# Four of 32 neighbour rows copied as columns of a turned table in SBUF, and a fifth fetched row by row by SyncE in two tiles of three

## The chip, the core and the metric

The kernel runs on one core of a Trainium2 chip. The metric is the device time of one execution in microseconds (us), of which the median over several runs is given. A core has five engines that run their own instruction queues beside each other: TensorE (PE in the profile), VectorE (DVE), ScalarE (ACT), GpSimd (POOL) and SyncE (SP). SP issues DMA transfers and computes nothing; POOL issues the indirect ones, whose source rows are named by a list of indices in SBUF.

## What is computed

The reference scores each of 16,384 users by a history of 100 items. Ahead of that, for each of 50,001 items and two tables of 32 values, it attends over the rows of the item's 32 neighbours:

```python
def _neighbor_attn(E, near_full):
    V = E[near_full]                      # [items, 32 neighbours, 32]
    scores = jnp.einsum('nd,nkd->nk', E, V) / jnp.sqrt(jnp.float32(GEO_HALF))
    w = jax.nn.softmax(scores, axis=-1)
    return jnp.einsum('nk,nkd->nd', w, V)
a_sus = _neighbor_attn(E_in, near_full)
a_inf = _neighbor_attn(E_out, near_full)
```

Then come the user scores, over rows `[E_hist, a_sus, a_inf]` of the history and `[E_tgt, a_inf, a_sus]` of the target, a hidden layer of 128 with relu, an exponential with a mask, a weighted sum over everything and a sigmoid for each user. All of it is in float32.

## The kernel before, in words

There are two stages, one after the other.

The item stage works on the rows of `egeo`, which has both tables side by side: 64 values, 256 bytes an item, `ROWS` = 50,048 items with the padding. A tile is 128 items, one in each partition; 17 tiles (`NSUB`) form an iteration, and there are 23 iterations, `NT` = 391 tiles. `load` brings an iteration's neighbour lists (`nidx`), own rows (`own`) and `ehist` rows (`row`) by SP; it is called in the middle of the iteration before. `gather(s)` issues 32 indirect transfers on POOL for tile s, one for each neighbour number k: each brings 128 rows of 64 values into `v[:, k]`. `v` has five buffers.

The arithmetic of a tile is spread over three steps of the loop over s. The loop writes out the order of the instructions on ACT, DVE and SP by hand (`manual_schedule`). In step s, DVE first does the weighted sum of tile s-2 (`weighted` twice, `attend`, `attended`), then the products and scores of tile s-1 (`products`, `scores`, `largest`). ACT copies the own rows of tile s-1 into PSUM (`even`) and takes the exponents of its scores (`exponents`). `finish(s-3)` completes a row, and at the end of an iteration writes the finished rows to two tables in DRAM (`table`, `ttab`) through ACT's queue.

The user stage follows: for each of 128 groups of 128 users and each of 100 places in the history, POOL gathers 128 rows of `table` (`h`), TensorE turns them, DVE multiplies them by the target's row, TensorE and ACT do the hidden layer and TensorE the scores. The change doesn't touch it.

In step s of the item stage the order is:

```python
gather(s)
if two:
    weighted(s - 2, 0); weighted(s - 2, 1); attend(s - 2); attended(s - 2)
if one:
    even(s - 1); products(s - 1); scores(s - 1); largest(s - 1); exponents(s - 1)
if three:
    finish(s - 3)
```

Of the kernel before, what the change touches and what calls it, by code (L numbers as in the profile page):

```python
# [22 lines left out]
DE = 64  # L23
# [8 lines left out]
NSUB = 17  # L32
NITER = -(-ITEMS // (P * NSUB))
ROWS = NITER * P * NSUB

# [17 lines left out]
def kernel(  # L53
# [13 lines left out]
    nc = tc.nc  # L67

    const = ctx.enter_context(tc.tile_pool(name="const", bufs=1))
# [31 lines left out]
    nc.scalar.dma_start(ttab[0 : ITEMS - 1, 0:DE], etgt[0 : ITEMS - 1, :])  # L104
    nc.scalar.dma_start(ttab[ITEMS - 1 : ITEMS, 0:DE], etgt[ITEMS - 1 : ITEMS, :])
    with (
        tc.manual_schedule(engines={E.Activation, E.DVE, E.SP}),
        tc.tile_pool(name="n_in", bufs=2) as n_in,
        tc.tile_pool(name="n_v", bufs=5) as n_v,
        tc.tile_pool(name="n_s", bufs=3) as n_s,  # L110
        tc.tile_pool(name="n_ps", bufs=2, space=bass.MemoryType.PSUM) as n_ps,
        tc.tile_pool(name="n_pb", bufs=1, space=bass.MemoryType.PSUM) as n_pb,
    ):
        its = {}
        subs = {}

        def load(it):
            nidx = n_in.tile([P, NSUB, K], I32, name="nidx")
            nc.sync.dma_start(nidx, near_v[it])
            own = n_in.tile([P, NSUB, 2 * G], F32, name="own")  # L120
            nc.sync.dma_start(own, egeo_v[it])

            row = n_in.tile([P, NSUB, W + G], F32, name="row")
            nc.sync.dma_start(row[:, :, 1 : 1 + DE], ehist_v[it])

            its[it] = (nidx, own, row)

        def gather(s):  # L130
            it, j = divmod(s, NSUB)
            nidx = its[it][0]
            v = n_v.tile([P, K, 2, G], F32, name="v")
            subs[s].update(v=v)
            for k in range(K):
                nc.gpsimd.indirect_dma_start(  # L136
                    out=v[:, k].rearrange("p t d -> p (t d)"),
                    out_offset=None,
                    in_=egeo,
                    in_offset=bass.IndirectOffsetOnAxis(ap=nidx[:, j, k : k + 1], axis=0),  # L140
                )

        def even(s):
            it, j = divmod(s, NSUB)
            own_ps = n_ps.tile([P, 1, 2 * G], F32, name="own_ps")
            nc.scalar.copy(own_ps[:, 0, :], its[it][1][:, j, :])
            subs[s]["own"] = own_ps

        def products(s):
            v = subs[s]["v"]  # L150
            prod = n_pb.tile([P, K * 2 * G], F32, name="big")
            prod = prod.rearrange("p (k t d) -> p k t d", k=K, t=2)
            nc.vector.tensor_tensor(  # L153
                prod.rearrange("p k t d -> p k (t d)"),
                v.rearrange("p k t d -> p k (t d)"),
                subs[s]["own"].to_broadcast([P, K, 2 * G]),
                ALU.mult,
            )
            subs[s]["prod"] = prod

        def scores(s):
            sc = n_s.tile([P, 2, K], F32, name="sc")
            nc.vector.tensor_reduce(  # L163
                sc.rearrange("p t k -> p k t"), subs[s]["prod"], AX.X, ALU.add
            )
            subs[s]["sc"] = sc

        def largest(s):
            sc = subs[s]["sc"]
            top = n_s.tile([P, 2], F32, name="top")  # L170
            nc.vector.tensor_reduce(top, sc, AX.X, ALU.max)
            nc.vector.tensor_scalar(top, top, -scale, None, ALU.mult)  # L172
            subs[s]["sc"] = (sc, top)

        def exponents(s):
            sc, top = subs[s]["sc"]
            ex = n_ps.tile([P, 2, K], F32, name="ex")
            tot = n_s.tile([P, 2, 1], F32, name="tot")
            for t in range(2):
                nc.scalar.activation(  # L180
                    ex[:, t, :],
                    sc[:, t, :],
                    AF.Exp,
                    bias=top[:, t : t + 1],
                    scale=scale,
                    accum_out=tot[:, t, :],
                )
# [14 lines left out]

        def attend(s):
            tot = subs[s]["ex"][1]
            nc.vector.reciprocal(tot, tot)
            att = n_s.tile([P, 2, G], F32, name="att")
            nc.vector.tensor_reduce(att, subs[s]["wv"], AX.X, ALU.add)  # L207
            subs[s]["att"] = att
# [12 lines left out]
        def finish(s):  # L221
            it, j = divmod(s, NSUB)
            row = its[it][2]
            nc.scalar.copy(row[:, j, W : W + G], row[:, j, 1 + DE : 1 + DE + G])
# [12 lines left out]

        NT = NITER * NSUB
        load(0)
        for s in range(NT + 3):  # L240
            if s < NT:
                if s % NSUB == NSUB // 2 and s // NSUB + 1 < NITER:
                    load(s // NSUB + 1)
                subs[s] = {}
                gather(s)
            one, two, three = (0 <= s - d < NT for d in (1, 2, 3))
            if two:
                weighted(s - 2, 0)
                weighted(s - 2, 1)
                attend(s - 2)  # L250
                attended(s - 2)
# [186 lines left out]
    with (  # L438
# [5 lines left out]
        part = f_s.tile([P, UC], F32, name="part")  # L444
# [6 lines left out]
        s = f_s.tile([P, 1], F32, name="s")  # L451
# [72 lines left out]
```

## Time and profile before

| what | value |
|---|---|
| median of 3 runs | 36178.12 us (36170.38 to 36182.2) |
| span of the profiled execution, first to last instruction | 31861.9 us |
| POOL busy | 24005.6 us, 25446 instructions |
| DVE busy | 6716.4 us |
| PE busy | 11868.8 us, nearly all in the user stage |
| mean granted TensorE clock | 0.905 |

The median lies 4316 us above the span of the profiled execution. The profile gives no time of that execution other than its span.

The profile is one execution as the hardware recorded it. A row of a group of instructions reads: line, engine, operation, output<-inputs, partitions x elements, count | busy us, mean ns of one | idle us of the engine just before them, and what ended most of it. A row of the timeline reads: start in us, duration in us, engine, line, operation, count [idle before it <- what ended it]. "SPq" is SP's queue of transfers. A row of waits reads: engine, tile and line <- what ended the wait: us in total, times, longest. "PEld" is TensorE's loading of weights.

### The profile page before, as it was taken

To read this page: it belongs to the slowest core of one execution; us is meant where nothing else is said; L and a number is where in the kernel's file an instruction comes from. 1 tells how busy PE (TensorE), PEld (TensorE's weight loads), DVE (VectorE), ACT (ScalarE), POOL (GpSimd) and SP (SyncE) were. 2 spreads that over 40 slices of the span, in tenths; PEclk is the share of its full clock that TensorE was granted. 3 is DMA by queue.
4 is the path that set the end of the run, shared out by engine and by line. 5 is a ranking of instruction groups with operands and counts; after the bars stand their busy time and mean duration, and the time that the engine had idled before them with its cause. 6 is when DMAs were issued, how large, how long until landed. Compare 5 with 4: busy or idle time off the path is not lost.

```text
span 31861.9 us, 106268 instructions
## 1 busy us (share of the span) xinstructions
PE 11868.8 (37%) x26243; PEld 3178.4 (10%) x26243; DVE 6716.4 (21%) x11111; ACT 2745.2 (9%) x6067; POOL 24005.6 (75%) x25446
## 2 busy tenths in 40 slices
PE   0000000000000000000277777777777777777777
PEld 0000000000000000000011111111111111111111
DVE  2222222222222222222211111111111111111111
ACT  0000000000000000000011111111111111111111
POOL 7777777777777777777777777777777777777777
PEclk9999999999999999999988888888888888888888
DMA  2111111111111111111122222222222222222222
GB/s 50 30 30 30 30 31 33 30 30 30 30 31 33 30 30 30 30 31 31 37 54 54 54 54 54 54 54 54 54 54 54 54 54 54 54 54 54 54 53 52
DMA packets 1027971, 1362.44 MB, mean 43 GB/s; under 512 B 559904, under 2 KB 614432, under 8 KB 1027360
## 3 DMA queue, kind: packets, MB, share of 16 engines
q0 software_dynamic: 814080, 1265.42, 19.7%
q10 hardware_dynamic: 151056, 51.51, 1.0%
q1 hardware_dynamic: 62224, 38.72, 0.5%
q8 instruction: 217, 3.56, 0.0%
q14 instruction: 394, 3.23, 0.0%
HBM read 1315.31 MB, written 51.50 MB: 43 GB/s over the span
## 4 chain that ended last, share of the span: by engine, by line
POOL 56%; issue 27%; DMA 9%; PE 7%; DVE 1%; POOLq 0%; ACT 0%; ACTq 0%; SPq 0%; DVEq 0%
POOL v L136 35%; POOL h L332 21%; DMA h<-table,hidx 6%; PE turned L372 3%; DMA v<-in_egeo_dram,nidx 3%; PE z_ps L363 3%; PE hT_ps L346 1%; POOL t L296 0%; DVE xT L351 0%; DVE ea L404 0%; DVE den L403 0%; DVE num L405 0%; DVE ea L402 0%; DVE hsum L354 0%; DMA table<-row 0%
## 5 line engine op out<-in xcount | busy, mean ns | idle before, releaser
L332 POOL DMA_INDIRECT h<-table,hidx x12800 | 12080.4, 944 | 3901.8 <-issue 3587.3
L136 POOL DMA_INDIRECT v<-in_egeo_dram,nidx x12512 | 11803.8, 943 | 3860.2 <-issue 3723.3
L308 PE MATMUL hT_ps<-ident,t 128*128 128x128 f32 x128 | 46.7, 365 | 15689.8 <-DMA hidx<-in_history_dram 15689.8
L346 PE MATMUL hT_ps<-ident,h 128*128 128x128 f32 x12800 | 3926.4, 350 | 4284.2 <-DMA h<-table,hidx 4186.4
L351 DVE TENSOR_TENSOR xT<-hT_ps,tT 128x512 f32<-128x512 f32 x3200 | 2213.9, 692 | 13113.0 <-PE hT_ps L346 13109.7
L372 PE MATMUL turned<-z,w_row 128*25 128x512 f32 x6400 | 4560.1, 805 | 0.0
L363 PE MATMUL z_ps<-xT,w1T 128*128 128x512 f32 x6400 | 4300.2, 761 | 0.0
L365 ACT ACTIVATE z<-z_ps,b_sb 128x512 f32<-128x512 f32 x3200 | 2199.7, 687 | 13823.9 <-PE z_ps L363 13823.9
L153 DVE TENSOR_TENSOR big<-v,own_ps 128x2048 f32<-128x2048 f32 x391 | 897.9, 2296 | 11251.8 <-DMA v<-in_egeo_dram,nidx 11251.5
L346 PEld LDWEIGHTS hT_ps<-ident,h 128*128 128x128 f32 x12800 | 1779.4, 154 | 9334.4 <-DMA h<-table,hidx 5701.4
L308 PEld LDWEIGHTS hT_ps<-ident,t 128*128 128x128 f32 x128 | 19.2, 150 | 15842.7 <-issue 15841.9
L180 ACT ACTIVATE ex<-sc,top 128x32 f32<-128x32 f32 x782 | 227.7, 291 | 15155.2 <-DVE top L172 15142.5
L363 PEld LDWEIGHTS z_ps<-xT,w1T 128*128 128x128 f32 x6400 | 1343.1, 255 | 3.1 <-ACT z L365 3.1
L194 DVE TENSOR_TENSOR big<-v,ex 128x1024 f32<-128x1024 f32 x782 | 960.6, 1228 | 355.5 <-ACT ex L180 342.0
L163 DVE TENSOR_REDUCE sc<-big 128x64 f32<-128x2048 f32 x391 | 896.4, 2293 | 13.4
L207 DVE TENSOR_REDUCE att<-big 128x64 f32<-128x2048 f32 x391 | 895.8, 2291 | 0.0
L372 PEld LDWEIGHTS turned<-z,w_row 128*25 128x25 f32 x6400 | 458.8, 115 | 3323.6 <-issue 3323.6
L354 DVE COPY hsum<-h 128x4 f32<-128x4 f32 x3200 | 528.5, 165 | 0.0
L296 POOL DMA_INDIRECT t<-ttab,tidx x128 | 120.8, 943 | 66.0 <-issue 37.8
L180 ACT ACTIVATION_READ_ACCUMULATOR ex<-sc,top 128x1 f32 x782 | 145.8, 186 | 0.0
L310 DVE COPY tT<-hT_ps 128x128 f32<-128x128 f32 x128 | 37.4, 292 | 262.4 <-PE hT_ps L308 262.4
L214 DVE TENSOR_TENSOR row<-att,tot 128x64 f32<-128x64 f32 x391 | 88.2, 226 | 13.3
(55 smaller groups left out, 1008.1 us busy)
## 6 DMA issues: line engine op xcount, KB each, us to landing
h<-table,hidx POOLq DMA_INDIRECT x12800, 2.6
v<-in_egeo_dram,nidx POOLq DMA_INDIRECT x12512, 2.4
table<-row ACTq DMA_DIRECT2D x22, 1096.5 KB, 13.4
own<-in_egeo_dram SPq DMA_DIRECT2D x23, 544.0 KB, 4.0
row<-in_ehist_dram SPq DMA_DIRECT2D x23, 544.0 KB, 4.9
ttab<-in_etgt_dram ACTq DMA_DIRECT2D x1, 12500.0 KB, 54.2
ttab<-row ACTq DMA_DIRECT2D x22, 544.0 KB, 4.6
hidx<-in_history_dram SPq DMA_DIRECT2D x32, 200.0 KB, 2.5
```

The costliest lines, as they stand in the source:

```text
L136: nc.gpsimd.indirect_dma_start(out=v[:, k].rearrange("p t d -> p (t d)"), out_offset=None, in_=egeo, in_offset=bass.IndirectOffsetOnAxis(a ...
L153: nc.vector.tensor_tensor(prod.rearrange("p k t d -> p k (t d)"), v.rearrange("p k t d -> p k (t d)"), subs[s]["own"].to_broadcast([P, K, ...
L163: nc.vector.tensor_reduce(sc.rearrange("p t k -> p k t"), subs[s]["prod"], AX.X, ALU.add)
L194: nc.vector.tensor_tensor(subs[s]["wv"][:, t].rearrange("p d k -> p k d"), subs[s]["v"][:, :, t, :], subs[s]["ex"][0][:, t, :] .rearrange( ...
L207: nc.vector.tensor_reduce(att, subs[s]["wv"], AX.X, ALU.add)
L332: nc.gpsimd.indirect_dma_start(out=rows[s][:, q, :], out_offset=None, in_=table, in_offset=bass.IndirectOffsetOnAxis(ap=users[c]["hidx"][: ...
L346: nc.tensor.transpose(hT[s][:, q, :], rows[s][:, q, 1:W], ident)
L351: nc.vector.tensor_tensor(xT[s], hT.pop(s), users[c]["tT"].to_broadcast([D, LG, P]), ALU.mult)
L354: copy = nc.vector.tensor_copy(users[c]["hsum"][:, g * LG : (g + 1) * LG], rows.pop(s)[:, :, 0:1].rearrange("p q o -> p (q o)"),)
L363: nc.tensor.matmul(z_ps, w1T, xT.pop(s), start=True, stop=True)
L365: nc.scalar.activation(z[s], z_ps, AF.Relu, bias=b1_sb)
L372: nc.tensor.matmul(users[c]["turned"], w2_row[:, NG - 1 - g : 2 * NG - 1 - g], of.rearrange("h q p -> h (q p)"), start=g == 0, stop=g == N ...
```

## The change

Tables of columns. `cols`, 128 partitions x 25,088 values (98 KB a partition), is laid out in SBUF. In partitions 0 to 63 its column i holds the 64 values of item i, in partitions 64 to 127 those of item i + 25,088 (`HALF`). `table_of_columns` fills it during the first six tiles (`WARM`): SP loads blocks of 128 rows, TensorE turns them, and DVE and ACT by turns copy 512 columns out of PSUM.

Addresses. Once in an iteration `addresses` turns the numbers of the last five neighbours (k = 27 to 31) of each item into byte addresses: a row's offset in DRAM for k = 27, a column's address in SBUF for the others, with `mark` telling the half. TensorE turns them, so that a tile's 128 addresses for one k lie in one partition, where a sequencer can load 16 of them into registers at once (`RUN`).

From tile 6 on, `gather(s)` issues 28 indirect transfers, or 27 where s is not divisible by three. The four columns k = 28 to 31 of a tile are 512 single columns of 128 values: DVE copies 256 of them (`by_dve`, k = 28 and 29), ACT 224, and TensorE the last 32 as products of the identity with one column (`by_pe`, two runs, `PEB`), which ACT then copies out of PSUM. `Columns.some` loads the registers of the next run before it issues the 16 copies of the present one. In the next step TensorE turns the 4 x 128 columns back into rows (`turned`), ACT copies the lower half's 64 values into `v` (`lower`), and DVE overwrites those of items in the upper half (`upper`, a predicated copy).

In two tiles of three SP fetches the rows of k = 27 one by one (`single_rows`): 128 transfers of 256 bytes, the source address in a register.

The work is interleaved by hand: `products`, `scores` and `attend` are cut into two parts each, and a run of 16 copies of DVE stands behind each of the eight large operations; the other eight runs follow at the end of the step. ACT does two runs, `lower` and `even`, eight runs, `exponents`, and the last four runs. `own` and `ex` share one PSUM tile, since the new tiles `vt` and `pc` take PSUM banks.

Built, the program has 1,796 indirect transfers fewer on POOL (10,716 in the item stage), 98,560 copies of one column more on DVE, 86,240 on ACT, 12,320 products of one column on TensorE, 14,368 loads of 16 registers, and 32,768 transfers of one row on SP. The transfers of SP use eight semaphores in turn: each waits until the one eight places before it has landed.

```diff
+HALF = -(-ROWS // (2 * P)) * P
+KC = 4
+KS = K - KC - 1
+KA = KC + 1
+RUN = 16
+WARM = 6
+PEB = 2
...
+        def columns_at(eng, s, q):
+            it, j = divmod(s, NSUB)
+            k, i = divmod(q * RUN, P)
+            r = j * KA + 1 + k
+            _, vals = nc.values_load_multi_w_load_instructions(
+                marks[it][1][r : r + 1, i : i + RUN],
+                engines=[eng],
...
+        def single_rows(s):
...
+            for i in range(0, P, RUN):
+                _, vals = nc.values_load_multi_w_load_instructions(
+                    marks[it][1][r : r + 1, i : i + RUN],
+                    engines=[E.SP],
...
+                for q, a in enumerate(vals):
...
+                    nc.sync.dma_start(
+                        v[i + q : i + q + 1, KS].rearrange("p t d -> p (t d)"),
+                        flat[:, ds(a // 4, DE)],
+                    )
+
+        class Columns:
...
+            def some(self, n=1):
+                for _ in range(n):
+                    if self.ready is None:
+                        if not self.runs:
+                            return
+                        self.ready = (self.runs[0], columns_at(self.eng, self.s, self.runs.pop(0)))
+                    q, vals = self.ready
+                    self.ready = None
+                    if self.runs:
+                        self.ready = (self.runs[0], columns_at(self.eng, self.s, self.runs.pop(0)))
+                    for i, a in enumerate(vals):
+                        self.put(q, i, a)
...
-            for k in range(K):
+            for k in range(K if s < WARM else KS if fetched(s) else KS + 1):
                 nc.gpsimd.indirect_dma_start(
...
+        def fetched(s):
+            return s >= WARM and s % 3 != 0
...
+        def turned(s):
+            vt = n_pc.tile([P, 4, P], F32, name="vt")
+            for k in range(KC):
+                nc.tensor.transpose(vt[:, k, :], subs[s]["cb"][k // 2][:, k % 2, :], ident)
+            subs[s]["vt"] = vt
+
+        def lower(s):
+            nc.scalar.copy(
+                subs[s]["v"][:, K - KC : K].rearrange("p k t d -> p k (t d)"),
+                subs[s]["vt"][:, :, 0:DE],
+            )
...
+            def by_dve(q, i, a):
+                k, o = divmod(q * RUN + i, P)
+                nc.vector.tensor_copy(cb[0][:, k, o : o + 1], cols[:, ds(a, 1)])
+
+            def by_act(q, i, a):
+                k, o = divmod(q * RUN + i - 2 * P, P)
+                nc.scalar.copy(cb[1][:, k, o : o + 1], cols[:, ds(a, 1)])
+
+            def by_pe(q, i, a):
+                o = (q - (2 * half - PEB)) * RUN + i
+                nc.tensor.matmul(
+                    pc[:, 0, o : o + 1], ident, cols[:, ds(a, 1)], start=True, stop=True
+                )
...
+            late = one and s - 1 >= WARM
+            if late:
+                turned(s - 1)
+            if WARM <= s < NT:
+                dve, act, pe = columns(s)
+            pe.some(PEB)
+            act.some(2)
+            if late:
+                lower(s - 1)
             if one:
                 even(s - 1)
-                products(s - 1)
-                scores(s - 1)
+            act.some(8)
+            if two:
+                for t in range(2):
+                    weighted(s - 2, t)
+                    dve.some()
+                for t in range(2):
+                    attend(s - 2, t)
+                    dve.some()
+                attended(s - 2)
+            if late:
+                upper(s - 1)
+            if one:
+                for part in range(2):
+                    products(s - 1, part)
+                    dve.some()
+                for part in range(2):
+                    scores(s - 1, part)
+                    dve.some()
                 largest(s - 1)
                 exponents(s - 1)
+            act.some(99)
+            dve.some(99)
+            if WARM <= s < NT and PEB:
+                n = PEB * RUN
+                nc.scalar.copy(subs[s]["cb"][1][:, 1, P - n : P], subs[s]["pc"][:, 0, 0:n])
```

More of the change, by code (lines that the diff above doesn't have):

```diff
@@ L106 @@
     with (
-        tc.manual_schedule(engines={E.Activation, E.DVE, E.SP}),
+        tc.manual_schedule(engines={E.Activation, E.DVE, E.SP, E.PE}),
+        tc.tile_pool(name="n_e", bufs=6) as n_e,
+        tc.tile_pool(name="n_c", bufs=2) as n_c,
         tc.tile_pool(name="n_in", bufs=2) as n_in,
@@ new lines, in columns_at @@
+        def columns_at(eng, s, q):
[5 more added lines that the diff above has]
+                engines=[eng],
+                min_val=base,
+                max_val=base + 4 * (HALF - 1),
+                skip_runtime_bounds_check_because="an item's number within its half, times 4",
+            )
+            return [
+                (
+                    v.with_bounds(
+                        min_val=base,
+                        max_val=base + 4 * (HALF - 1),
+                        guaranteed_mod_val=0,
+                        out_of_modulus=4,
+                    )
+                    - base
+                )
+                // 4
+                for v in vals
+            ]
@@ L141, in gather @@
                 )
+        def fetched(s):
+            return s >= WARM and s % 3 != 0
         def even(s):
             it, j = divmod(s, NSUB)
[L145 to L149, printed above, removed]
-            v = subs[s]["v"]
-            prod = n_pb.tile([P, K * 2 * G], F32, name="big")
-            prod = prod.rearrange("p (k t d) -> p k t d", k=K, t=2)
+            oe = n_ps.tile([P, 2, 2 * G], F32, name="oe")
+            nc.scalar.copy(oe[:, 0, :], its[it][1][:, j, :])
+            subs[s]["own"] = oe[:, 0:1, :]
+            subs[s]["ex_ps"] = oe[:, 1, :].rearrange("p (t k) -> p t k", t=2)
@@ L153, in products @@
+        def products(s, part):
+            v = subs[s]["v"]
+            if part == 0:
+                big = n_pb.tile([P, K * 2 * G], F32, name="big")
+                subs[s]["prod"] = big.rearrange("p (k t d) -> p k t d", k=K, t=2)
+                subs[s]["sc"] = n_s.tile([P, 2, K], F32, name="sc")
+            ks = slice(part * K // 2, (part + 1) * K // 2)
             nc.vector.tensor_tensor(
-                prod.rearrange("p k t d -> p k (t d)"),
-                v.rearrange("p k t d -> p k (t d)"),
@@ L201, in weighted, with attend @@
             )
[L203 to L208, printed above, removed]
+        def attend(s, t):
+            if t == 0:
+                tot = subs[s]["ex"][1]
+                nc.vector.reciprocal(tot, tot)
+                subs[s]["att"] = n_s.tile([P, 2, G], F32, name="att")
+            nc.vector.tensor_reduce(
+                subs[s]["att"][:, t : t + 1], subs[s]["wv"][:, t : t + 1], AX.X, ALU.add
+            )
         def attended(s):
@@ L238, with columns, some @@
         NT = NITER * NSUB
+        groups = -(-blocks // 4)
         load(0)
+        def columns(s):
+            cb = [n_c.tile([P, 2, P], F32, name=n) for n in ("cd", "ca")]
+            subs[s]["cb"] = cb
+            half = 2 * P // RUN
+            pc = n_pc.tile([P, 4, P], F32, name="pc")
+            subs[s]["pc"] = pc
+            def by_dve(q, i, a):
[8 more added lines that the diff above has]
+                    pc[:, 0, o : o + 1], ident, cols[:, ds(a, 1)], start=True, stop=True
+                )
+            return (
+                Columns(E.DVE, s, range(half), by_dve),
+                Columns(E.Activation, s, range(half, 2 * half - PEB), by_act),
+                Columns(E.PE, s, range(2 * half - PEB, 2 * half), by_pe),
+            )
+        class Nothing:
+            def some(self, n=1):
+                pass
         for s in range(NT + 3):
+            dve = act = pe = Nothing()
             if s < NT:
```

106 lines of the change are left out of this document (94 added, 12 removed).

## The prediction

> **What bounds the kernel now.** I read the page first: busy shares, then the chain of waits.
>
> ```profile
> span 31861.9 us, 106268 instructions
> PE 11868.8 (37%) x26243; PEld 3178.4 (10%) x26243; DVE 6716.4 (21%) x11111; ACT 2745.2 (9%) x6067; POOL 24005.6 (75%) x25446
> POOL 56%; issue 27%; DMA 9%; PE 7%; DVE 1%; POOLq 0%; ACT 0%; ACTq 0%; SPq 0%; DVEq 0%
> L136 POOL DMA_INDIRECT v<-in_egeo_dram,nidx x12512 | 11803.8, 943 | 3860.2 <-issue 3723.3
> ```
>
> POOL is busy for 75%, and most of the rest of the chain is "issue", the gap in which POOL waits for nothing. The item stage's gathers are L136. Their timeline gives what one costs with its gap:
>
> ```profile
> 9.88 1.10 POOL L136 DMA_INDIRECT v<-in_egeo_dram,nidx  x1 [8.57 <-DMA nidx<-in_near_dram]
> ...
> 15664.44 0.94 POOL L136 DMA_INDIRECT v<-in_egeo_dram,nidx  x1 [0.30 <-issue]
> ```
>
> 12,511 steps in 15,654.56 us are 1.2513 us each; 32 make a tile of 40.04 us. The waits and the windows show that the other engines follow:
>
> ```profile
> DVE big L153 <- DMA v<-in_egeo_dram,nidx: 11251.5, 390, 30.3
> ACT ex L180 <- DVE top L172: 15142.5, 391, 39.6
> 60.00:15660.00 15600.00, 0.00 (x0) 0.00 (x0) 3947.88 (x3531) 410.16 (x2338) 11761.74 (x12468) 1.00 0.17 31
> ```
>
> The windows' columns are PE, PEld, DVE, ACT, POOL. Over 390 tiles DVE works 10.12 us and ACT 1.05 us a tile, and PE nothing. DVE waits 28.9 us a tile for gathers. This idle time is what the change spends.
>
> **What is removed.** From tile 6 on, POOL gathers 28 columns in tiles divisible by three (129 tiles) and 27 in the other 256: 10,716 gathers in place of 12,512. 1,796 x 1.2513 = 2,247 us, if POOL stays the bound. POOL's mean over the 385 tiles becomes 27.34 x 1.2513 = 34.2 us. Every other engine has to stay below 34.2 a tile for the whole gain, and below 40.04 for any.
>
> **DVE.** 256 copies of 128x1 a tile with the source column in a register, 16 loads of 16 registers, a predicated copy, and three big operations cut in two. No row has a register address. The nearest is the small copy L354:
>
> ```profile
> L354 DVE COPY hsum<-h 128x4 f32<-128x4 f32 x3200 | 528.5, 165 | 0.0
> 15889.42 0.16 DVE L354 COPY hsum<-h 128x4 f32<-128x4 f32 x1
> 15889.49 0.26 DVE L402 TENSOR_TENSOR ea<-ea,keep 128x100 f32<-128x100 f32 x1
> L310 DVE COPY tT<-hT_ps 128x128 f32<-128x128 f32 x128 | 37.4, 292 | 262.4 <-PE hT_ps L308 262.4
> ```
>
> It lasts 0.165 us, but the next operation starts 0.07 us after it: neighbours overlap. Bounds: 0.07 and 0.165. I take 0.07, since the copies depend on nothing and stand in rows of 16: 17.9 us. The fixed work becomes 10.1 + 3 x 0.07 + about 0.45 (predicated copy of 256 elements out of PSUM, by L310 and 128 elements more) + 0.3 (the address work, once in 17 tiles) = 11.1 us.
>
> **The register loads.** No row shows one. Below stands a sequencer's own instruction, above the shortest landing of a DMA:
>
> ```profile
> L292 SPq EVENT_SEMAPHORE  x148: 17/28/1356, 15667.0 to 29818.4; - x148
> L292 SPq DMA_DIRECT2D hidx<-in_history_dram x32: 327/328/617, 15692.2 to 29819.7; - x32
> out_dram<-res SPq DMA_DIRECT2D x1, 64.0 KB, 1.6
> ```
>
> So 0.03 to 1.6 us. I take 0.45, nearest to the 0.33 us in which SP's sequencer handles one transfer, plus something for the read. Each load is for the next run; on DVE eight of 16 stand behind an operation of about 1.1 us, which hides them; without that cover they cost 3.6 us more. The other eight cost 3.6. DVE: 17.9 + 11.1 + 3.6 = 32.6 us; ends 29.2 (loads nearly free) to 66 (0.165 a copy, eight loads at 1.6 us).
>
> [...]
>
> **ACT.** 224 copies, 14 loads, a copy of 256 elements out of PSUM and one of 32.
>
> ```profile
> 6025.01 0.20 ACT L224 COPY row<-row 128x32 f32<-128x32 f32 x1
> 6025.12 0.20 ACT L146 COPY own_ps<-own 128x64 f32<-128x64 f32 x1
> L382 ACT COPY by_g<-turned 25x512 f32<-25x512 f32 x128 | 71.5, 558 | 2.9 <-PE turned L372 2.9
> ```
>
> Spacing 0.11 (a 32-element copy), length 0.20: 24.6 to 45 us; I take 0.11. With 1.05 + 0.35 + 0.2 fixed and 14 x 0.45 of loads: 32.5 us. What is new behind a wait: `exponents` stands after ten runs and waits for DVE's `largest`; behind it wait four runs, the copy of PE's columns and `finish`, and for these PE's turning of the next step. DVE reaches `largest` after 8 runs (9.0) and nearly all fixed work, at about 20 us of its step; ACT's ten runs end at about 17.6 + 4.5 = 22. The wait is late for nobody.
>
> **PE.** 32 one-column products and four turnings.
>
> ```profile
> L450 PE MATMUL s_ps<-psum,ones 128*128 128x1 f32 x2 | 0.6, 346 | 6.2 <-DVE psum L448 6.2
> L450 PEld LDWEIGHTS s_ps<-psum,ones 128*128 128x128 f32 x2 | 0.5, 309 | 6.2 <-issue 6.2
> ```
>
> 36 x (0.35 + 0.31) = 24 us at most, on an engine idle here. Hidden; uncovered it would be added to ACT's 32-column copy and the turning.
>
> **SP.** In 256 tiles 128 transfers of one row, and 8 loads with nothing in front of them.
>
> ```profile
> 0.75 0.38 SPq L85 DMA_DIRECT2D b_sb<-in_b_dram  x1
> 1.19 0.42 SPq L87 DMA_DIRECT2D w_sb<-in_w_dram  x1
> 1.66 0.55 SPq L89 DMA_DIRECT2D w_sb<-in_w_dram  x1
> ```
>
> These rows start 0.44 and 0.47 us apart; L292 above takes 0.33. Those have 128 rows to describe, the new ones one, so 0.47 is the upper bound; the lower is 0.2, since in the built program each transfer waits for the one eight before it to land, and the shortest landing is 1.6 us. I take 0.37 (L292 and a gap of 0.04): 47.4 + 3.6 = 51 us, over three tiles two of these, 34.0 a tile. The ends are 17 (0.2, loads at 0.03) and 49 (0.47, loads at 1.6). Five `v` buffers let SP run ahead in the tile without rows, so that the mean over three tiles counts. SP's loads of `nidx`, `own` and `row` now queue behind the rows, but are issued nine tiles before their use, some 300 us; a late one would stop POOL and, in `addresses`, DVE.
>
> **Tables at the start.** 98 transfers, 196 transposes and 49 PSUM copies of 512 elements run beside six tiles of 40 us; by L382 25 copies are 14 us an engine. Hidden; uncovered some 30 us.
>
> **Sum.** POOL 34.2, SP 34.0, DVE 32.6, ACT 32.5: POOL still sets the pace, but by very little. The profiled span becomes 31,862 - 2,247 = 29,615, plus about 70 us for steps in which one of four nearly equal engines comes late: 29,685. The median of 36,178 stands 4,316 above the profiled span; no row shows this time, so I leave it as it is: 36,178 - 2,177 = **34,000 us**. Were it spread in proportion (36,178 / 31,862 = 1.1355), the gain would be 2,551 and the time 33,627. A measurement here can tell 0.2% (72 us) from no change.
>
> **Rivals.**
> 1. The pace passes to one of the other three, short of 40.04. At 36.5 us a tile the gain is 3.5 x 385 = 1,360: 34,820. For it: three sums within 2 us of POOL's. Against: each would have to be well above its nearest row.
> 2. Slower: DVE's register copies can't be started ahead like L354's. It decides from (40.04 - 11.1 - 3.6) / 256 = 0.099 us a copy, midway between spacing and length. At 0.115: 44.1 us, + 1,560: 37,740; at 0.165 and no overlap 56.9 us: 42,700. For it: no row shows such an instruction. ACT's own point is (40.04 - 7.9) / 224 = 0.143.
> 3. Slower by the loads: each holds its sequencer for the 1.6 us landing and nothing hides it: 16 x 1.6 + 17.9 = 43.5 us, with the big operations beside the loads: + 1,330, 37,510. [...]
> 4. No gain: SP's transfers keep the 0.44 us spacing: (56.3 + 3.6) x 2/3 = 39.9 us: 36,140.
> 5. The change doesn't do what it says: gathers get dearer beside DVE's many copies. From 1.465 us (40.04 / 27.34) nothing is left. Against: L332 runs beside L354 in the second stage at the same 0.94.
>
> ```profile
> L332 POOL DMA_INDIRECT h<-table,hidx x12800 | 12080.4, 944 | 3901.8 <-issue 3587.3 <-PE turned L372 159.1 <-PE hT_ps L346 97.8
> ```
>
> **How the numbers follow.** Forecast 0.40 (33,550 to 34,500), rival 1 0.23, rival 2 0.24, rival 3 0.07, rivals 4 and 5 0.06, of which 0.04 are no change. Faster: 0.40 + 0.23 + 0.01 = 0.64; same 0.04; slower 0.32. Below 33,550 I leave 0.02; the upper end at 37,500 takes in rivals 1, 4 and the mild half of 2 and leaves 0.17.
>
> **What will show it.** L136's successor with 10,716 gathers, still 1.25 us apart with "issue" before them, and POOL first in the chain: right. Gathers that wait for DVE or ACT to free `v`: rival 1 or 2; then the spacing of the 128x1 copies decides (0.07 or above 0.099), and any hole of over 0.5 us between runs is the load. A wait of `products` for SP's rows points to SP. The first 240 us and the second stage should look as before. Wrong altogether: gathers above 1.4 us.

## The result, and the profile after

| | runs | median us | lowest to highest |
|---|---|---|---|
| before | 4 | 36,178.12 | 36,170.38 to 36,182.2 |
| after | 4 | 44,176.83 | 44,133.84 to 44,222.77 |

The ratio is 1.2212, with a 95% interval of 1.2194 to 1.2229: the change makes the kernel 22% slower, and the predicted 34,000 us is 10,200 us off. The page of the profiled execution of the changed kernel (44,210.67 us), with busy time and mean length of one behind the bar, and idle time and what ended it last:

```profile
span 44208.5 us, 432721 instructions
PE 15785.9 (36%) x52642; PEld 8822.8 (20%) x52642; DVE 13938.0 (32%) x111416; ACT 12380.8 (28%) x93101; POOL 22308.3 (50%) x23650
L267 POOL DMA_INDIRECT v<-in_egeo_dram,nidx x10716 | 10110.0, 943 | 15299.6 <-DVE big L353 12017.1
L416 ACT COPY ca<-cols 128x1 f32 x86240 | 9483.7, 187 | 13676.4 <-issue 13595.4
L412 DVE COPY cd<-cols 128x1 f32 x98560 | 7315.0, 145 | 11213.0 <-issue 10623.1
```

POOL is down from 75% to 50%. A gather still takes 943 ns, there are 10,716 of them as planned, and yet POOL stands idle for 15,300 us before them, mostly until DVE has done its last product of an older tile and a `v` buffer is free. So DVE is late. But DVE is busy for only 32%, and what it waits for before its small copies is "issue": nothing that the profile shows. ACT has the same.

Before the two traces are compared, one number of the prediction has to be put right. The page shown there had a span of 31,862 us, the timed runs 36,178. A second execution of the unchanged kernel, profiled beside the experiments below, took 36,322 us, like the timed ones. Its page and its windows (columns PE, PEld, DVE, ACT, POOL, granted clock, DMA share, GB/s):

```profile
span 36320.2 us, 106268 instructions
L136 POOL DMA_INDIRECT v<-in_egeo_dram,nidx x12512 | 13320.4, 1065 | 4176.0 <-issue 4081.4
```

```profile
0.00:17510.00 17510.00, 0.45 (x1) 0.18 (x1) 3960.95 (x3543) 412.77 (x2346) 13321.05 (x12518) 1.00 0.16 28
17510.00:36320.00 18810.00, 10060.81 (x26242) 3152.57 (x26242) 2734.17 (x7569) 2295.83 (x3721) 12197.40 (x12928) 0.73 0.21 46
```

The 4,316 us are inside the program, in both stages, and not around it. The item stage ends at 17,500 us instead of 15,665; its gathers are 1.398 us apart in the mean, where the first page had 1.251. All that follows is compared with this execution. The same windows for the changed kernel:

```profile
0.00:25500.00 25500.00, 5783.44 (x26332) 5682.13 (x26332) 11175.40 (x103564) 10060.76 (x89173) 10110.72 (x10722) 0.50 0.10 19
25500.00:44208.00 18708.00, 10002.44 (x26310) 3140.65 (x26310) 2762.63 (x7853) 2320.04 (x3929) 12197.56 (x12928) 0.73 0.21 46
```

The second stage is as long as before (18,708 and 18,810 us). The whole loss, some 7,900 us, is in the item stage: its last gather starts at 25,410 us instead of 17,497.

What happens there shows in the timeline of one tile. POOL's rows first (start, length, what was done, idle time before it):

```profile
8102.86 0.94 POOL L267 DMA_INDIRECT v<-in_egeo_dram,nidx  x1 [68.34 <-DVE big L353]
8104.11 0.94 POOL L267 DMA_INDIRECT v<-in_egeo_dram,nidx  x1 [0.31 <-issue]
...
8136.55 0.94 POOL L267 DMA_INDIRECT v<-in_egeo_dram,nidx  x1 [0.30 <-issue]
8165.68 0.94 POOL L267 DMA_INDIRECT v<-in_egeo_dram,nidx  x1 [28.18 <-DVE big L353]
```

28 gathers run in one burst, 1.25 us apart, and then POOL waits 28 us for a buffer. DVE and ACT in the same stretch:

```profile
8104.66 1.05 DVE L412 COPY cd<-cols 128x1 f32 x16
8105.63 1.21 DVE L367 TENSOR_REDUCE att<-big 128x32 f32<-128x1024 f32 x1
...
8118.41 0.15 DVE L412 COPY cd<-cols 128x1 f32 x1 [0.16 <-issue]
8119.81 0.15 DVE L412 COPY cd<-cols 128x1 f32 x1 [1.24 <-issue]
8121.21 0.15 DVE L412 COPY cd<-cols 128x1 f32 x1 [1.25 <-issue]
...
8139.42 0.15 DVE L412 COPY cd<-cols 128x1 f32 x1 [1.25 <-issue]
8140.81 1.23 DVE L311 TENSOR_TENSOR big<-v,oe 128x1024 f32<-128x1024 f32 x1 [1.24 <-issue]
8142.21 1.06 DVE L412 COPY cd<-cols 128x1 f32 x16 [0.17 <-issue]
```

```profile
8118.40 0.19 ACT L416 COPY ca<-cols 128x1 f32 x1 [1.19 <-issue]
8119.80 0.19 ACT L416 COPY ca<-cols 128x1 f32 x1 [1.21 <-issue]
8121.20 0.19 ACT L416 COPY ca<-cols 128x1 f32 x1 [1.21 <-issue]
```

Until some 4 us after the first gather DVE starts 16 copies in 1.05 us. For the next 11 us one or two copies start every 0.7 or 1.4 us, and from 8118 us on each copy stands alone, 1.40 us after the last, and ACT's copies come at the same instants. It ends at 8142 us, 3.5 us after the last packet of the gathers' queue has ended (8138.7 us in the trace's DMA records), and at once 16 copies take 1.06 us again. SP's part as single records of the trace (start us, length ns), inside and after a burst:

```
8119.087   699  MOVE            8143.192    29  MOVE
8120.486   700  DMA_DIRECT2D    8143.251   225  DMA_DIRECT2D
8121.886   701  MOVE            8143.512    29  MOVE
8123.288   709  DMA_DIRECT2D    8143.571   225  DMA_DIRECT2D
```

Even a MOVE, whose record names neither a semaphore nor memory, takes 0.70 us instead of 0.03, and the next instruction begins a further 0.70 us later. PE is held back too: a weight load and a matmul together take 2.8 us there (matmuls start at 8,119.1, 8,121.9 and 8,124.7 us). So once this burst of gathers has run for some 15 us (from 8,118 us on), every engine but POOL starts one instruction in 1.40 us. This state is called the stall below. DVE's 265 instructions a tile (103,564 in 391 tiles; at 1.40 us each 371 us), and its loads, can't be started under 34 us of gathers; POOL runs out of free buffers, stops, and DVE and ACT do their work in the pause. The two times, which the change meant to lay side by side, are added: a step takes 62.6 us (median) where it took 44.8.

### The profile page after: what moved, and what is told of

Its sections match the earlier page's. It is cut to its first block, busy times and chain, and to the rows that moved or that the text cites. A ratio compares the mean times of both kernels' runs of the same rounds, so it can differ in the third digit from the quotient of the medians.

```text
span 44208.5 us, 432721 instructions
## 1 busy us (share of the span) xinstructions
PE 15785.9 (36%) x52642; PEld 8822.8 (20%) x52642; DVE 13938.0 (32%) x111416; ACT 12380.8 (28%) x93101; POOL 22308.3 (50%) x23650
## 5 line engine op out<-in xcount | busy, mean ns | idle before, releaser
L267 POOL DMA_INDIRECT v<-in_egeo_dram,nidx x10716 | 10110.0, 943 | 15299.6 <-DVE big L353 12017.1
L416 ACT COPY ca<-cols 128x1 f32 x86240 | 9483.7, 187 | 13676.4 <-issue 13595.4
L412 DVE COPY cd<-cols 128x1 f32 x98560 | 7315.0, 145 | 11213.0 <-issue 10623.1
L420 PE MATMUL pc<-cols,ident 128*128 x24640 | 5227.9, 340 | 3867.1 <-issue 3828.2
L420 PEld LDWEIGHTS pc<-cols,ident 128*128 128x128 f32 x24640 | 5391.8, 330 | 3441.5 <-issue 3407.3
L603 PE MATMUL turned<-z,w_row 128*25 128x512 f32 x6400 | 4054.3, 721 | 0.0
L577 PE MATMUL hT_ps<-ident,h 128*128 128x128 f32 x12800 | 2361.1, 312 | 584.4 <-DVE xT L582 365.4
L311 DVE TENSOR_TENSOR big<-v,oe 128x1024 f32<-128x1024 f32 x782 | 959.2, 1227 | 500.3 <-issue 468.4
L353 DVE TENSOR_TENSOR big<-v,oe 128x1024 f32<-128x1024 f32 x782 | 953.4, 1219 | 2.1 <-ACT oe L339 2.0
L320 DVE TENSOR_REDUCE sc<-big 128x32 f32<-128x1024 f32 x782 | 950.1, 1216 | 0.2
L367 DVE TENSOR_REDUCE att<-big 128x32 f32<-128x1024 f32 x782 | 945.5, 1210 | 2.5 <-issue 2.5
```

Of the source, the lines that this page charges most:

```text
L267: nc.gpsimd.indirect_dma_start(out=v[:, k].rearrange("p t d -> p (t d)"), out_offset=None, in_=egeo, in_offset=bass.IndirectOffsetOnAxis(a ...
L311: nc.vector.tensor_tensor(subs[s]["prod"][:, ks].rearrange("p k t d -> p k (t d)"), v[:, ks].rearrange("p k t d -> p k (t d)"), subs[s]["o ...
L353: nc.vector.tensor_tensor(subs[s]["wv"][:, t].rearrange("p d k -> p k d"), subs[s]["v"][:, :, t, :], subs[s]["ex"][0][:, t, :] .rearrange( ...
L412: nc.vector.tensor_copy(cb[0][:, k, o : o + 1], cols[:, ds(a, 1)])
L416: nc.scalar.copy(cb[1][:, k, o : o + 1], cols[:, ds(a, 1)])
L420: nc.tensor.matmul(pc[:, 0, o : o + 1], ident, cols[:, ds(a, 1)], start=True, stop=True)
```

## The experiments

All runs stand here, one execution each, beside one of the unchanged kernel on the same chip (36,310 us for the first four, 36,296 for the second, 36,280 for the third). "Step" is the mean distance of `largest` from one tile to the next on DVE, from tile 9 on, with the median in brackets where it differs by more than 1 us. The item stage "ends" with the start of its last gather, in e7 and e11 with the last `largest`.

| run | whole us | item stage ends | step us |
|---|---|---|---|
| changed kernel | 44,211 | 25,410 | 65.2 (62.6) |
| b0_before_again | 36,322 | 17,497 | 44.8 |
| e1_no_sp_rows | 43,289 | 24,386 | 62.5 |
| e2_fixed_columns | 44,463 | 25,504 | 65.5 (56.3) |
| e3_wide_copies | 43,303 | 24,357 | 62.5 (76) |
| e4_64_tiny_act | 37,598 | 18,744 | 47.6 (64.1) |
| e5_9_wide_act | 36,306 | 17,502 | 44.8 |
| e6_wide_no_rows | 34,246 | 15,394 | 39.1 (40.6) |
| e7_queue_for_gathers | 33,313 | 14,507 | 36.7 (32.0) |
| e8_192_tiny_act | 40,913 | 21,982 | 56.0 |
| e9_half_by_queue | 36,826 | 17,895 | 45.8 |
| e10_half_height | 44,267 | 25,335 | 65.0 |
| e11_gpsimd_busy | 33,302 | 14,486 | 36.6 (32.0) |

The first page's execution shows no stall, so it matters that no run below is of its kind. The second stage, which no run changes, tells: from the last `largest` to the end it takes 16,190 us on the first page and 18,667 to 18,819 us in every run of the table.

### The kernel before, once more

> The kernel before, unchanged, for a second profile. The first profile's span is 31,862 us, the timed median 36,178. If the 4,316 us lie inside the program, the span comes out near 36,170, and the two stages (15,664 us and 16,168 us in the first profile) show which one holds them. If they lie outside, the span is 31,862 again.

It gave the span of 36,320 us read above, so the missing time is in the program.

### Which part of the change: SP's rows, the registers, or the number of copies

```
 def fetched(s):                                   # e1
-    return s >= WARM and s % 3 != 0
+    return False
```
```
-_, vals = nc.values_load_multi_w_load_instructions(...)   # e2, e3
...
+return [q * RUN + n for n in range(RUN)]          # e2
+return [q * RUN]                                  # e3
-nc.vector.tensor_copy(cb[0][:, k, o : o + 1], cols[:, ds(a, 1)])
+nc.vector.tensor_copy(cb[0][:, k, o : o + RUN], cols[:, ds(a, RUN)])   # e3, and so on ACT and PE
```

> The changed kernel without SyncE's one-row transfers: every tile from the seventh on has 28 gathers on POOL. In the changed kernel's trace every instruction on ACT, DVE and SP costs 1.40 us from about 5 us after a run of gathers begins until it ends, and 0.06 to 0.3 us outside. Theory A (the one-row transfers beside the gathers slow all queues): the 1.40 us are gone, DVE and POOL run beside each other, 35 to 38 us a tile, item stage 13,700 to 14,800 us instead of 25,410. Theory B (register addresses and register loads do it) and theory C (any dense instruction stream beside gathers does it): 60 to 66 us a tile as before, item stage about 24,000 to 25,500.

> The changed kernel with the columns' addresses fixed: the same 512 copies a tile on DVE, ACT and TensorE, but always of the same columns and without register loads on those engines (the four neighbours' values are not the item's own). SyncE's one-row transfers stay. Theory B: the 1.40 us are gone and a tile takes 34 to 37 us. Theories A and C: 58 to 66 us a tile, since SyncE's transfers and the number of instructions are as before.

> As the last, but each run of 16 copies is one instruction of 16 columns: 16 copies on DVE, 14 on ACT, 2 products on TensorE a tile (the four neighbours' values are not the item's own). SyncE's one-row transfers stay. Theory C: the pace comes back to POOL's or SyncE's, 34 to 38 us a tile. Theory A: SyncE's 128 transfers still meet the gathers, 1.40 us an instruction holds SyncE, and a tile stays above 45 us. Theory B: 34 to 37 us.

None of the three gets back more than 1,000 us of the 8,000. Without SP's rows the burst and the pause stay as they are:

```profile
L267 POOL DMA_INDIRECT v<-in_egeo_dram,nidx x10972 | 10373.1, 945 | 14012.2 <-DVE big L353 10775.4
```

What e1 does get back is the steps between two groups of 17 tiles: in the changed kernel 22 steps take 88 to 157 us, 1,049 us more than 22 median steps, and e1 has no such step past the start. With columns and addresses fixed (e2: no load on DVE, ACT or PE, no register in a copy) DVE's copies still stand 1.40 us apart in a burst, so neither dynamic addresses nor loads make the stall:

```profile
8106.41 0.15 DVE L390 COPY cd<-cols 128x1 f32<-128x1 f32 x1 [1.25 <-issue]
8107.81 0.15 DVE L390 COPY cd<-cols 128x1 f32<-128x1 f32 x1 [1.25 <-issue]
POOL v L245 <- DMA v<-in_egeo_dram: 6104.6, 133, 59.4
POOL v L245 <- DVE big L331: 6005.1, 249, 51.4
```

The mean step is the same, but that alone would say less: POOL's waits (the last two rows) are now as long for SP's rows as for DVE, so what the loads cost DVE can't be read from this run. With one copy for 16 columns (e3) DVE and ACT no longer have much to start, but SP still has 256 instructions in two tiles of three, and now these are late:

```profile
L245 POOL DMA_INDIRECT v<-in_egeo_dram,nidx x10716 | 10109.9, 943 | 14247.0 <-DMA v<-in_egeo_dram 8980.7
L390 DVE COPY cd<-cols 128x16 f32<-128x16 f32 x6160 | 788.8, 178 | 2.1 <-issue 2.1
```

The idle time before DVE's copies has gone from 11,213 us to 2, and POOL waits for SP's rows in place of DVE. Each part alone is enough to keep the stall, so taking one away shows little; what the parts share is many instructions beside the gathers.

### The number of instructions by itself

The unchanged kernel with copies of a constant into a scrap on ACT, which nothing reads and which leave PE, DVE and SP alone:

```
             if three:
                 finish(s - 3)
+            for n in range(64):                   # e8: range(192)
+                nc.scalar.copy(junk[:, n : n + 1], zeros[:, 0:1])
```
```
+            for n in range(9):                    # e5; junk and zeros are 128x512
+                nc.scalar.copy(junk, zeros)
```

> The kernel before, with 64 copies of one column (128x1) a tile added on ScalarE, from a constant to a scrap of SBUF that nothing reads; no other engine gets work. Their own time is 64 x 0.092 = 5.9 us a tile on an engine that is busy under 2 us of 44.8. Theory N (number of instructions: once gathers have run for some 10 us every engine starts one instruction per 1.40 us): 74 ScalarE instructions a tile do not fit, since 45 us of gathers leave room for 32; the other 42 wait until the gathers have stopped, 52 to 57 us a tile, item stage 20,300 to 22,300 us, whole 39,000 to 41,000 us. Theory W (the work of the copied columns sets the pace: DVE's, ScalarE's and TensorE's busy time, the turning, the waits for buffers): 36,250 to 36,400 us, as before. Theory C (TensorE's lower granted clock slows all): as before too, since TensorE does nothing here.

> The kernel before with 9 ScalarE copies of 128x512 a tile instead of the 64 tiny ones: the same 6 us of ScalarE work in a seventh of the instructions (19 in all a tile, under the 32 that fit). Theory N: 36,250 to 36,500 us. If ScalarE's busy time or its traffic beside the gathers were the cause: as slow as the 64 tiny copies, 39,000 us or more. Theory W: 36,250 to 36,400.

> The kernel before with 192 tiny ScalarE copies a tile, three times those of the first dose (192 x 0.093 = 17.9 us of work on that engine, still far under the 44.8 us tile). Theory N with alternation (few instructions of ScalarE start while rows of gathers arrive, so the gathers run out of buffers, stop, and the copies then run at 0.09 us): 32 x 1.25 = 40 us of gathers plus 10 us of tail and some 130 copies at 0.093 = 12: 55 to 62 us a tile, item stage 21,500 to 24,200, whole 40,200 to 43,000 us. If the cost is a small price for each instruction, as the first dose alone could be read (2.8 us for 64): 53.2 us a tile, 39,500 us. Theory W: 36,300 us.

Nine wide copies, some 6 us of ACT a tile, cost nothing (36,306). 64 tiny ones with as much work cost 1,300 us, and 192 cost 4,630, though ACT would be done with them in 18 of 44.8 us. The sizes agree only in part: e8 lies in the expected range (40,200 to 43,000), e4 well below its own (39,000 to 41,000); in a burst of e4 ACT ran at full speed for some 11 us (8,005 to 8,016) and then at 0.70 as well as at 1.40 us an instruction. With 64 POOL issues the 96 gathers of three tiles on end and then pauses for some 25 us, which is why the median step of e4 lies so far from its mean. Neither dose is a fixed price: 64 cost 2.8 us a step and 192 cost 11.2. ACT of e8 inside a burst (8078 to 8118 us), in the pause of POOL, and in the next burst, which begins at 8134 us:

```profile
8107.82 0.19 ACT L264 COPY junk<-zeros 128x1 f32<-128x1 f32 x1 [1.21 <-issue]
8109.22 0.19 ACT L264 COPY junk<-zeros 128x1 f32<-128x1 f32 x1 [1.21 <-issue]
...
8131.31 9.43 ACT L264 COPY junk<-zeros 128x1 f32<-128x1 f32 x100
8141.11 0.94 ACT L264 COPY junk<-zeros 128x1 f32<-128x1 f32 x9 [0.38 <-issue]
```

100 copies run in 9.43 us: they begin where POOL pauses and go on at that speed for the first 7 us of the next burst. PE does nothing in this item stage, and its granted clock is 1.00 there:

```profile
2000.00:20000.00 18000.00, 0.00 (x0) 0.00 (x0) 3227.49 (x2890) 7192.38 (x63193) 9642.33 (x10222) 1.00 0.12 22
```

So e8's stall needed no lower clock. Nor does a clock of 0.50, as in the changed kernel's item stage, bring it: e7, below, has that clock and no stall:

```profile
2000.00:14000.00 12000.00, 4965.22 (x22332) 4734.20 (x22332) 8659.65 (x88350) 7709.83 (x75942) 0.00 (x0) 0.50 0.14 31
```

### Few instructions, the rest of the change kept

e6 is e3 and e1 together: wide copies of fixed columns, no row by SP, 28 gathers.

> The changed kernel with one copy (one product) for each run of 16 columns, at fixed columns without registers, and with no row by SyncE: 28 gathers in every tile past the first six. It keeps the tables, the turning, the split products, the second PSUM tile, the TensorE products, and copies other columns than the right ones. Theory N: the pace is again near the gathers', 28 x 1.25 to 1.40 = 35 to 39 us, with some stall left 39 to 46 us a tile: item stage 15,300 to 18,000, whole 34,000 to 36,700 us. Theory W (the path of the copied columns, from turning to predicated copy, holds the buffers) or theory C (clock at 0.5): 55 to 63 us a tile as in the two runs that took only one of these away, 40,500 to 43,300 us.

```profile
L245 POOL DMA_INDIRECT v<-in_egeo_dram,nidx x10972 | 10546.9, 961 | 4846.4 <-issue 3252.1
POOL v L245 <- remote: 1379.5, 252, 15.7
```

34,246 us, 2,050 less than the unchanged kernel beside it: POOL sets the pace again, nine in ten of its gathers come 1.25 us apart, and tables, turning, predicated copy and products cost little. They and the 28 gathers of 35 us make a step of 39.1: in most of the remaining 4 us POOL waits for a buffer (the second row; "remote" is a release that the profile can't name). (12,512 - 10,972) x 1.40 = 2,156 us was to be expected from the gathers left out, and the item stage ended 2,103 us earlier, but this agreement is partly luck: the 1.40 of the unchanged kernel is a mean with slowed gathers, the 1.40 of this run one with pauses. It can't take the place of either kernel: the columns that the item stage needs lie apart, and the change copies each by an instruction of its own.

### What about the gathers does it

```
-nc.gpsimd.indirect_dma_start(out=v[:, k]..., in_=egeo, ...)           # e7
+for lo, hi in ((0, 43), (43, 86), (86, P)):
+    nc.sync.dma_start(v[lo:hi, k]..., egeo[k * P + lo : k * P + hi])
```
```
+nc.gpsimd.memset(scrap, 0.0)        # e11: e7, and this ahead of each three transfers
```
```
+if s >= WARM and k % 2:             # e9: e7's transfers for every second k
```
```
-out=v[:, k]...,                     # e10, past the first six tiles
+out=v[0:64, k]...,
+nc.sync.dma_start(v[64:P, k]..., egeo[k * P + 64 : k * P + P])
```

All four leave SP's single rows out and keep the tiny copies with their loads.

> The changed kernel without SyncE's rows, and with each gather of the item stage replaced by three plain transfers on SyncE's queue (43, 43 and 42 rows of a fixed block): the same bytes, rows and places, 84 transfers a tile at 0.32 to 0.40 us = 27 to 34 us, GpSimd idle. It loads other rows than the right ones. If the stall comes of the gather instruction on GpSimd: the 128x1 copies run at 0.06 and 0.09 us all the time, the tile takes what the slowest engine needs, 34 to 42 us: item stage 13,300 to 16,500, whole 32,000 to 35,200 us. If it comes of the rows in flight (or of what is recorded of them): the stalls stay, 50 to 65 us a tile, whole 38,000 to 44,000 us.

> The kernel with plain transfers on SyncE's queue in place of all gathers of the item stage, and one memset of 128x1024 on GpSimd beside each three transfers, so that GpSimd works in the whole item stage but moves no rows. If it is the gathers' rows or their descriptors that stall the others: as without the memsets, 33,300 us, or GpSimd's own pace if a memset is above 1.15 us. If a busy GpSimd alone stalls them: 50 us a tile or more, whole above 38,000 us, with 128x1 copies at 1.40 us in the trace.

> The changed kernel without SyncE's rows; past the first six tiles every second gather is replaced by three plain transfers of a fixed block on SyncE's queue (43, 43 and 42 rows): 14 gathers and 42 transfers a tile. The rows at odd places are other rows than the right ones. Theory N: a burst of 14 gathers lasts 17.5 us and the stall only sets in 5 to 15 us after its start, so little of it is left: 34 to 44 us a tile, item stage 13,500 to 17,400, whole 32,200 to 36,200 us. If any gather in flight is enough to hold the other engines back for its whole time: 45 us or more, whole above 36,500 us.

> The changed kernel without SyncE's rows; past the first six tiles each of the 28 gathers fetches rows for partitions 0 to 63 only, and one plain transfer on SyncE's queue fills partitions 64 to 127 from a fixed block (other rows than the right ones there). If the stall goes with the number of gather instructions on GpSimd: as long as with whole gathers, 58 to 65 us a tile, whole 41,500 to 44,300 us. If it goes with the rows that gathers have in flight, and a gather of 64 rows still takes near 1.25 us: half the rows arrive in each us, the stall is less than half as deep, 36 to 48 us a tile, whole 33,000 to 37,800 us. If a gather of 64 rows takes about half the time, rows arrive as fast as before, in bursts of 18 us: 36 to 48 us a tile too, and the spacing of the gathers tells the two apart.

With the same bytes brought by SP's queue in 84 transfers a tile, the tiny copies run at 0.061 us on DVE and 0.093 on ACT throughout (median spacing) and a step takes 32.0 us; every seventeenth takes near 109, in which ACT waits some 80 us, before it writes the finished rows, for a semaphore that SP's transfers raise. The idle time before DVE's copies is 2,189 us, where the changed kernel has 11,213:

```profile
L410 DVE COPY cd<-cols 128x1 f32 x98560 | 6508.2, 145 | 2188.7 <-issue 2177.3
L414 ACT COPY ca<-cols 128x1 f32 x86240 | 8492.7, 187 | 3058.4 <-issue 2882.6
```

A memset of 951 ns in the place of each gather, which keeps POOL as busy as gathers would, changes nothing:

```profile
L268 POOL MEMSET scrap<- 128x1024 f32 x10972 | 10435.0, 951 | 628.9
L416 ACT COPY ca<-cols 128x1 f32 x86240 | 8493.9, 187 | 3016.6 <-issue 2929.4
```

So neither a busy GpSimd nor rows that arrive by the other queue stall the engines. Half as many gathers take the step to 45.8 us, above the 34 to 44 that theory N gave, on the rival's side (36,826): the stall is there for the whole length of a burst of 14 too, but for its first 4 us. Gathers of half the height keep the step at 65.0. They carry half the bytes in as many packets (764,800 on the gathers' queue, as in e1) and last nearly as long:

```profile
L268 POOL DMA_INDIRECT v<-in_egeo_dram,nidx x10972 | 9917.8, 904 | 15417.0 <-DVE big L358 12082.8
```

So it was not the number of bytes that counted here (65.0 us a step with half of them, 62.5 in e1), but the number of gather instructions, or of their packets (45.8 us with half of them). The runs tell these two apart no further.

With the 32.0 us that the engines need without gathers, one sum comes near these runs: gathers of a tile x their spacing, and the engines' own step, less some 4 us at the start of a burst (less than 1 us in e10).

| run | gathers + engines | step | overlap |
|---|---|---|---|
| changed kernel | 27.34 x 1.25 + 32.0 = 66.2 | 62.6 | 3.6 |
| e1 | 28 x 1.25 + 32.0 = 67.0 | 62.5 | 4.5 |
| e9 | 14 x 1.25 + 32.0 = 49.5 | 45.6 (median) | 3.9 |
| e10 | 28 x 1.207 + 32.0 = 65.8 | 65.1 (median) | 0.7 |

By the same rows no other split of the copies would beat the kernel before, which is an estimate and wasn't run: one neighbour less saves a gather, 1.25 to 1.40 us, and its 128 copies take DVE and ACT together 128 / (1 / 0.061 + 1 / 0.093) = 4.7 us, most of which adds to the step.

## Why the prediction was wrong, point by point

- **The step that failed** is the line "POOL 34.2, SP 34.0, DVE 32.6, ACT 32.5: POOL still sets the pace". It took the largest of four sums, as if the engines started their instructions independently. In the changed kernel's traced execution they don't: beside the gathers DVE and ACT came down to one instruction in 1.40 us each, so the right form was POOL plus the slowest of the others. With the prediction's own terms that gives 34.2 + 34.0 = 68.2 us a step with SP, or 34.2 + 32.6 = 66.8 with DVE, which POOL was seen to wait for, less the 4; the trace has 62.6. No sum of an engine was far out; the way they were put together was.
- **The terms.** e7 shows the engines' step without gathers at 32.0 us against 32.6 predicted for DVE. Copies: 0.061 on DVE (0.07 taken) and 0.093 on ACT (0.11 taken). The load of 16 registers was mis-sized: 1.12 us on DVE, 1.03 on ACT and 1.25 on SP, the slowest, in the median of the changed kernel's trace, 0.45 taken. Part of it lies under the copies, since the next run's load is issued ahead of them: in e7 the hole between the last runs of a step is mostly 0.60 us, and the cheaper copies made up for the rest. PE's 32 products a tile are two matmuls and two weight loads each (24,640 of both in the trace), twice the number behind the prediction's 24 us; they stayed hidden all the same.
- **SP.** 0.32 us for a row outside a burst (0.37 taken), 2.8 inside: a move and a transfer at 1.40 each. Its transfers also cost the 1,049 us in the steps between groups. There ACT, before it writes the finished rows, waits for a semaphore that SP's transfers raise (at one such step it is idle for 102.6 us, until 3,636 us); the prediction named a late load of SP there, and put nothing on it.
- **The 4,316 us "left as it is".** This was the sign that was passed over. Nothing lay around the span; the profiled execution was another case than the timed ones, and in an execution of the timed length over four in ten gathers came 1.40 us or more after the last, with hardly any other instructions beside them. A page that is 12% off the time to be predicted isn't a page of that time.
- **Rivals.** Rival 5 had the right pair, gathers beside DVE's many copies, and the wrong direction: the copies got dearer, from 0.06 to 1.40 us, and the gathers kept 1.25. Rival 2 came nearest to the sign (copies above 0.099 us, DVE the bound) for a reason that isn't the one: with fixed columns the copies are as slow. (Its 0.099 lies nearer to the spacing of 0.07 than to the length of 0.165, not midway.) The sign given for "wrong altogether", gathers above 1.4 us, would have missed the case; that POOL waits for DVE to free `v` was named for rivals 1 and 2, and is what came.
- **What held.** Second stage unchanged, tables at the start hidden (tile 6 begins at 276 us instead of 249), PE hidden, 1,796 gathers fewer.

## What to carry to other kernels

Where one engine issues gathers back to back, don't take the idle time of the other engines as free for many small instructions: here 192 copies with 18 us of work on an idle ACT made a step of 44.8 us 11.2 us longer (e8). Count instructions, not busy time, and add the two sums unless a run has shown that they overlap. Few wide instructions fitted beside the gathers here (nine a tile in e5: 36,306 us beside 36,296; e6 had a step of 39.1 us for 35 us of gathers). When the profiled execution isn't of the same length as the timed ones, find out where the difference lies before anything is subtracted from it.

## What the runs showed of the hardware

The stall came in steps of 0.70 us, on DVE, ACT, SP and PE in the same stretch: on SP 0.70 from the start of an instruction to its end and 0.70 to the next start, as in its records above, while the copies keep their 0.15 us on DVE and 0.19 on ACT and start 1.40 us apart, on both at the same instants (8,119.81 and 8,119.80 us). It outlasted the gathers' packets, by 3.6 us in the median after bursts of 28 (e1) and by 1.7 after bursts of 14 (e9). POOL's own gathers show the same steps in the unchanged kernel, where they don't pause, in the execution of 36,322 us:

```profile
8032.61 0.96 POOL L136 DMA_INDIRECT v<-in_egeo_dram,nidx  x1 [0.30 <-issue]
8033.88 1.09 POOL L136 DMA_INDIRECT v<-in_egeo_dram,nidx  x1 [0.30 <-DMA v<-in_egeo_dram,nidx]
8035.28 1.10 POOL L136 DMA_INDIRECT v<-in_egeo_dram,nidx  x1 [0.30 <-issue]
8036.68 1.10 POOL L136 DMA_INDIRECT v<-in_egeo_dram,nidx  x1 [0.30 <-issue]
```

The gathers pass from 1.25 to 1.40 us, twice 0.70, and back again: 56% of the distances are below 1.3 us, 28% at 1.40 and 15% longer, up to 2.1 us in the main. The mean is 1.398: 12,511 x (1.398 - 1.251) = 1,840 us, which is what the item stage of this execution has more than on the first page. Why its second stage is 2,630 us longer than there (95% of its gathers come 1.25 us apart, the rest wait, mostly for 2 to 10 us) was not followed; the change leaves that stage as it is.

What makes the stall is not settled, and no run shows it. SP's MOVE took 0.70 us instead of 0.03, and the next instruction began a further 0.70 us later; rows by the gathers' queue were in flight then, and with the same bytes by SP's queue (e7) DVE's and ACT's copies stayed 0.061 and 0.093 us apart. Nor was it tried whether the recording of the trace has a part in it: no run is known to have gone without (the timed ones of the changed kernel too come with a span and a clock), and were it so, part of the loss would belong to the recording. Recording alone is not enough, though: the first page is a recorded execution of the same 106,268 instructions, and all but 30 of its 12,511 distances between gathers are below 1.3 us. What set that execution apart from the timed ones is not known. Whether it is the gather instruction or its packets that matter was not tried either.
